# Turned attention probabilities: from SBUF to SBUF in four transfers instead of through DRAM

## Chip, cores and metric

One core of a Trainium2 chip. The metric is the device time of one execution in microseconds (us), lower is better. The kernel before runs in 1198.78 us, the median of three runs (1196.74 to 1199.55).

## What is computed

A per-sequence LoRA matmul is added to the input, then attention with 32 query heads and 8 key/value heads over a paged cache of 512 keys plus the 128 new ones, and its output projection is added too. Eight sequences of 128 tokens; everything is float32. Cut to what matters:

```python
x = x + einsum('bsi,boi->bso', x, weight[adapter_ids])          # LoRA, 512 x 512
q = rope(rmsnorm(einsum('bsd,ed->bse', x, Wq)))                  # 8 x 128 x 32 x 128
k = rope(rmsnorm(einsum('bsd,ed->bse', x, Wk)))                  # 8 x 128 x  8 x 128
v = einsum('bsd,ed->bse', x, Wv)
kc, vc = k_cache[block_table], v_cache[block_table]              # 512 cached keys
k_all, v_all = concat([kc, k]), concat([vc, v])                  # 640 keys
scores = einsum('bqhd,bkhd->bhqk', q, k_all) * SCALE             # each kv head serves 4 q heads
scores = where(valid, scores, -1e30)
probs = softmax(scores)
o = einsum('bhqk,bkhd->bqhd', probs, v_all)
x = x + einsum('bse,de->bsd', o, Wo)
```

## The kernel before

**Tiling.** The heads are cut into G = 4 groups of 2 key/value heads and 8 query heads. A *step* i is one group for one sequence: 32 steps, group by group, and in each group the eight sequences. A step has 8 *slots* h, one per query head. The four query heads that share a key/value head j (0 or 1) are a *unit* (i, j), so slots 0 to 3 and 4 to 7 make one unit each, 64 units in all.

**One slot.** TensorE computes the scores of one head, 128 queries x 640 keys (line 1031). VectorE adds the mask, takes the row minimum and moves them to SBUF (line 1041), ScalarE takes the exponential and its row sum (1057), VectorE the reciprocal (1098), GpSimd scales (1105). This gives p, 128 queries on the partitions x 640 keys.

**Turning the probabilities.** The product with the values needs the keys on the partitions. So in the next slot VectorE turns p in blocks of 32 x 32 (`turn_p`, line 871), into the quarter of the tile tp that belongs to that head. A turned block still has its rows on the wrong partitions: block b of 32 query rows lies on partitions 32b to 32b + 31, each with four pieces (a = 0 to 3) of 640 floats, 2,560 bytes. What is wanted is pT: piece a of partition 32b + i at partition 4i + a, in column block b. Before, two transfers on the SP queue do this. `send(u)` (line 887) writes tp to a DRAM tile xp, 128 partitions x 10,240 bytes, whose addresses run so that (i, a) becomes one index. `receive(u)` (line 894) reads it back, 128 partitions x 4 pieces of 2,560 bytes. The loop calls `send` in the slot of the unit's last turn (line 1065), puts `receive` in the list `to_read`, and calls it one slot later (1073 to 1077), after the `receive` of q if there is one. Keys, queries and later groups' weights go through DRAM in the same manner (xk and kT, xq and qT on SP; tw, xw and w on the ACT queue). Of the last unit the turns are done by TensorE, so 63 units take this way.

**Buffers.** tp has two. pT has one for both units of a step in steps 0 to 4; from step 5 on the second unit uses the buffer that held the LoRA weights, so each of the two has its own. xp has three.

**Order.** The order on each engine is written out by hand. What TensorE does beside the scores stands in `main` for each step: the projections of step i + 1 (`pj_kv`, `pj_q`), `values(i - 1, j)` (o from pT, line 559), `output(i - 1)` and, in the first group, the LoRA product. The pieces are spread over the eight slots. From step 6 on, pT of a unit (i, 0) is read around slot 2 of step i + 1 and pT of (i, 1) around slot 4.

**Queues.** SP only issues transfers, in program order: what stands behind a transfer that waits, waits too. ACT (ScalarE) issues the weights' transfers in between its own arithmetic, and they hold that up in the same way. Each of the 552 transfers of SP and ACT takes the next of eight completion signals, in the order in which the program was laid out over both queues, and before it is issued it waits until the transfer eight places before it, the last on the same signal, has landed. The gathers on GpSimd's queue have signals of their own.

**Weights.** The weights of group g + 1 are turned during group g. In the last two steps of a group, ACT reads them back into the tiles w_kv and w_q (line 517, `receive_weights`) as soon as the old ones have been used, and TensorE uses w_q about two slots after its last row was asked for.

Of the kernel before, what the change touches and what calls it, by code (L numbers as in the profile page):

```python
# [11 lines left out]
FP = mybir.dt.float32  # L12
# [6 lines left out]
P = 128  # L19
# [6 lines left out]
REP = HQ // HK  # L26
# [4 lines left out]
Q4 = P // 4  # L31
NC = LA // P
QK = LA // 4
# [19 lines left out]
def lora_then_paged_attention(  # L53
# [18 lines left out]
    nc = tc.nc  # L72
# [3 lines left out]
    def pool(name, bufs=1, **kw):  # L76
        return ctx.enter_context(tc.tile_pool(name=name, bufs=bufs, **kw))
# [14 lines left out]
    xch = pool("xch", 3, space=bass.MemoryType.DRAM)  # L92
# [686 lines left out]

    to_read = []  # L780

    def send_k(i):
        s = st[i]
        tk = work.tile([P, 4, GK, LC * Q4], FP, tag="tk", name=f"tk_{i}")
        for j in range(GK):
            nc.vector.transpose(
                tk[:, :, j, :].rearrange("p a (c k) -> p a c k", c=LC),
                s.kc[:, :, j * D : (j + 1) * D].rearrange("p c (a d) -> p a c d", a=4),
            )
        s.xk = xch.tile([4, P, GK, LC * Q4], FP, tag="xk", name=f"xk_{i}")  # L790
        nc.sync.dma_start(
            out=s.xk.rearrange("b (i a) h x -> (b i) (a h x)", a=4),
            in_=tk.rearrange("p a h x -> p (a h x)"),
        )
# [9 lines left out]
    def send_q(i, n):  # L804
        s = st[i]
        tq = work.tile([P, 4, 4, Q4], FP, tag=f"tq{n}", name=f"tq_{i}_{n}")
        nc.vector.transpose(tq, s.q[n].rearrange("p h (a d) -> p a h d", a=4))
        xq = xch.tile([4, P, 4, Q4], FP, tag=f"xq{n}", name=f"xq_{i}_{n}")
        nc.sync.dma_start(
            out=xq.rearrange("b (i a) h q -> (b i) (a h q)", a=4),  # L810
            in_=tq.rearrange("p a h q -> p (a h q)"),
        )

        def receive():
            s.qT[n] = work.tile([P, 4, 4, Q4], FP, tag=f"qT{n}", name=f"qT_{i}_{n}")
            nc.sync.dma_start(
                out=s.qT[n].rearrange("d b h q -> d b (h q)"),
                in_=xq.rearrange("b d h q -> d b (h q)"),
            )

        to_read.append((now[0], 0, receive))
# [46 lines left out]
    def turn_p(u, r):  # L868
        if r == 0:
            u.tp = turned.tile([P, 4, REP, QK], FP, tag="tp", name=f"tp_{u.i}_{u.j}")  # L870
        nc.vector.transpose(u.tp[:, :, r, :], u.p.pop(r).rearrange("q (a k) -> q a k", a=4))  # L871
# [12 lines left out]
            t[:, 0:LA].rearrange("p (c b q) -> p c b q", c=NC, b=4),  # L884
        )

    def send(u):
        u.scr = xch.tile([4, P, REP * QK], FP, tag="xp", name=f"xp_{u.i}_{u.j}")
        nc.sync.dma_start(
            out=u.scr.rearrange("b (i a) x -> (b i) (a x)", a=4),  # L890
            in_=u.tp.rearrange("p a r k -> p (a r k)"),
        )

    def receive(u):

        pl, tag = (lora, "raw") if u.j and u.i >= B - 3 else (pts, "pT")
        pT = pl.tile([P, 4, REP, QK], FP, tag=tag, name=f"pT_{u.i}_{u.j}")
        nc.sync.dma_start(
            out=pT.rearrange("p b r k -> p b (r k)"), in_=u.scr.rearrange("b p x -> p b x")
        )  # L900
        st[u.i].pT[u.j] = pT

    def run(queue):
        calls = list(queue)
        queue.clear()
        for f in calls:
            f()
# [73 lines left out]
    for i, (g, b) in enumerate(steps):  # L981
# [38 lines left out]
        for h in range(8):  # L1020
            j, r = h // 4, h % 4
# [8 lines left out]
            for lo, hi in ((0, L), (L, LA)):  # L1030
# [7 lines left out]
            p = probs.tile([P, LA], FP, tag="p", name=f"p_{i}_{h}")  # L1038
# [3 lines left out]
                out=p,  # L1042
# [17 lines left out]
            if prev is not None:  # L1060
                u, pr = prev
                if u.i < last or u.j == 0:
                    turn_p(u, pr)
                if pr == REP - 1:
                    send(u)
                    to_read.append((8 * i + h, 1, lambda u=u: receive(u)))
            run(later)
            run(to_write)
            if 8 * i + h in turn_when:
# [10 lines left out]
            if h == (1 if i else 3) and i < last:  # L1080
                send_k(i + 1)
# [7 lines left out]
            while main and (h == 7 or took + main[0][0] / 2 <= share):  # L1089
                cost, f = main.pop(0)  # L1090
# [9 lines left out]
            if i == last and j == 1:  # L1100

                unit.p[r] = probs.tile([P, LA], FP, tag="p", name=f"pk_{h}")
                p = p.rearrange("q (a c i) -> q a c i", a=4, c=NC)
# [79 lines left out]
```

## Time and profile before

| | before |
|---|---|
| median of three runs | 1198.78 us (1196.74 to 1199.55) |
| the profiled execution | 1197.03 us |
| its span, first to last instruction | 1194.7 us |
| granted TensorE clock | 1.00 |
| busy: VectorE / ScalarE / GpSimd | 61% / 44% / 56% of the span |
| DMA engines, mean busy share by queue | SP and ACT's q1 59.6% and q10 12.4%, GpSimd's q0 10.1% |
| moved | 328.02 MB in 187148 packets; HBM read 195.04 MB, written 132.12 MB |
| one step, first group | about 41 us |
| one step, other groups | 34.6 us |

The profile is one execution on the chip. PE is TensorE's matmuls, DVE is VectorE, ACT ScalarE, POOL GpSimd, SP the engine that only issues transfers; a name ending in q is an engine's queue of issues. L1041 is line 1041 of the kernel. An arrow points from what is read to what is written. In a list of waits, the columns are: who waited, for what, us in total, how many times, the longest. In a timeline, the first column is the start in us from the start of the span and the second the duration; for a transfer that is the time its issue took, not its landing. A row of windows has the stretch, its length, PE's busy time, the granted clock, the DMA share and GB/s. A list of DMA issues ends with the median us from issue to landing.

### The profile page before, as it was taken

To read this page: it belongs to the slowest core of one execution; us is meant where nothing else is said; L and a number is where in the kernel's file an instruction comes from. 1 tells how busy PE (TensorE), PEld (TensorE's weight loads), DVE (VectorE), ACT (ScalarE), POOL (GpSimd) and SP (SyncE) were. 2 spreads that over 40 slices of the span, in tenths; PEclk is the share of its full clock that TensorE was granted. 3 is DMA by queue.
4 is the path that set the end of the run, shared out by engine and by line. 5 is a ranking of instruction groups with operands and counts; after the bars stand their busy time and mean duration, and the time that the engine had idled before them with its cause. 6 is when DMAs were issued, how large, how long until landed. Compare 5 with 4: busy or idle time off the path is not lost.

```text
span 1194.7 us, 12971 instructions
## 1 busy us (share of the span) xinstructions
PE 1178.0 (99%) x3412; PEld 576.4 (48%) x3412; DVE 733.6 (61%) x1675; ACT 531.5 (44%) x1648; POOL 674.9 (56%) x781
## 2 busy tenths in 40 slices
PE   7899999999999999999999999999999999999998
PEld 4554455454444444444444444444444444444454
DVE  5566656665566666766566676666657655565651
ACT  4564444444444444444444444444444444444432
POOL 5566455545566556555655556565556556655540
PEclk9999999999999999999999999999999999999999
DMA  8388788877988988888998998888898987777761
GB/s 290 110 278 273 261 292 293 275 261 246 309 289 301 334 303 300 294 270 300 296 303 280 340 313 298 298 278 300 267 319 277 303 285 264 243 255 242 260 222 60
DMA packets 187148, 328.02 MB, mean 275 GB/s; under 512 B 13124, under 2 KB 106052, under 8 KB 178116
## 3 DMA queue, kind: packets, MB, share of 16 engines
q1 hardware_dynamic: 124272, 239.23, 59.6%
q10 hardware_dynamic: 49524, 48.12, 12.4%
q0 software_dynamic: 13280, 39.86, 10.1%
q8 instruction: 27, 0.44, 0.2%
q14 instruction: 45, 0.37, 0.1%
HBM read 195.04 MB, written 132.12 MB: 274 GB/s over the span
## 4 chain that ended last, share of the span: by engine, by line
PE 97%; DMA 1%; ACT 1%; DVE 0%; POOL 0%; issue 0%; ACTq 0%; DVEq 0%; POOLq 0%
PE o L559 23%; PE sc L1031 23%; PE pj_q L559 18%; PE out L559 18%; PE pj_kv L559 9%; PE y L559 2%; PE lw L474 1%; DMA w_q<-xw_q 1%; PE x L474 1%; PE kt L763 1%; PE wt_q L492 0%; PE wt_kv L492 0%; PE qt L772 0%; PE wt_o L492 0%; PE pt L881 0%
## 5 line engine op out<-in xcount | busy, mean ns | idle before, releaser
L1041 DVE CUSTOM_DVE_ANT_0 p<-sc,mask 128x640 f32<-128x640 f32 x256 | 210.9, 824 | 400.5 <-PE sc L1031 400.4
L1057 ACT ACTIVATE p<-p,mn 128x640 f32<-128x640 f32 x256 | 211.6, 827 | 324.6 <-DVE mn L1041 322.4
L1031 PE MATMUL sc<-kT,qT 128*128 128x512 f32 (+1 forms) x1024 | 318.4, 433 | 1.1 <-ACT kT L764 0.8
L1105 POOL TENSOR_SCALAR p<-p,rc 128x640 f32<-128x640 f32 x252 | 201.9, 801 | 183.0 <-DVE rc L1098 181.0
L1031 PEld LDWEIGHTS sc<-kT,qT 128*128 128x128 f32 x1024 | 189.9, 190 | 226.4 <-issue 206.0
L559 PE MATMUL pj_q<-w_q,x1T 128*128 128x512 f32 x512 | 236.9, 593 | 1.4 <-ACT w_q L493 0.7
L559 PE MATMUL o<-pT,vc 128*128 128x512 f32 x512 | 236.9, 593 | 0.0
L559 PE MATMUL out<-w_o,oT 128*128 128x512 f32 (+1 forms) x528 | 234.9, 580 | 0.9 <-ACT oT L838 0.7
L871 DVE STREAM_TRANSPOSE tp<-p 128x640 f32<-128x640 f32 x252 | 211.0, 837 | 4.9 <-POOL p L1105 4.7
L610 POOL DMA_INDIRECT kc<-in_L_cond_k_cache_dram,key_ix x128 | 130.8, 1022 | 32.7 <-issue 32.5
L610 POOL DMA_INDIRECT vc<-in_L_cond_v_cache_dram,val_ix x128 | 127.9, 999 | 31.0 <-issue 30.8
L692 ACT ACTIVATE q<-q,rs 128x128 f32<-128x128 f32 x256 | 81.9, 390 | 139.1 <-POOL q L679 134.5
L559 PEld LDWEIGHTS out<-w_o,oT 128*128 128x128 f32 x528 | 95.7, 190 | 93.5 <-issue 89.9
L559 PEld LDWEIGHTS pj_q<-w_q,x1T 128*128 128x128 f32 x512 | 92.4, 190 | 93.8 <-issue 91.4
L559 PEld LDWEIGHTS o<-pT,vc 128*128 128x128 f32 x512 | 91.9, 190 | 88.6 <-issue 81.3
L559 PE MATMUL pj_kv<-w_kv,x1T 128*128 128x512 f32 x256 | 116.6, 593 | 0.7 <-ACT x1T L476 0.7
L671 POOL TENSOR_TENSOR k<-sw 128x256 f32<-128x256 f32 x31 | 22.9, 739 | 157.1 <-PE kt L763 133.4
L679 POOL TENSOR_TENSOR q<-q,sw 128x512 f32<-128x512 f32 x59 | 74.7, 1266 | 45.0 <-DVE sw L662 44.9
L646 ACT ACTIVATE sq<-pj_q 128x128 f32<-128x128 f32 x256 | 70.8, 277 | 50.4 <-PE pj_q L559 41.5
L687 POOL TENSOR_TENSOR rs<-ss,mhalf 128x6 f32<-128x6 f32 x64 | 77.6, 1212 | 5.3
L559 PEld LDWEIGHTS pj_kv<-w_kv,x1T 128*128 128x128 f32 x256 | 45.9, 190 | 45.6 <-issue 44.7
L559 PE MATMUL o<-pT,vn 128*128 128x512 f32 x128 | 65.4, 593 | 0.0
(123 smaller groups left out, 873.6 us busy)
## 6 DMA issues: line engine op xcount, KB each, us to landing
xp<-tp SPq DMA_DIRECT2D x63, 1280.0 KB, 5.9
pT<-xp SPq DMA_DIRECT2D x63, 1280.0 KB, 7.0
xk<-tk SPq DMA_DIRECT2D x31, 512.0 KB, 7.5
kT<-xk SPq DMA_DIRECT2D x62, 256.0 KB, 6.6
xq<-tq SPq DMA_DIRECT2D x59, 256.0 KB, 4.6
qT<-xq SPq DMA_DIRECT2D x59, 256.0 KB, 5.2
st_q<-in_L_cond_Wq_dram ACTq DMA_DIRECT2D x24, 256.0 KB, 5.3
xw_q<-tw_q ACTq DMA_DIRECT2D x24, 256.0 KB, 4.4
```

The lines of the kernel that those rows point to most:

```text
L474: nc.tensor.transpose(t[:, j, :], blk, ident)
L559: nc.tensor.matmul(y[0], lhsT=lhsT, rhs=rhs, start=(k == 0), stop=(k == len(pieces) - 1))
L610: nc.gpsimd.indirect_dma_start(out=dst[:, c, :], out_offset=None, in_=src, in_offset=bass.IndirectOffsetOnAxis(ap=rows[:, g, at : at + 1], ...
L646: nc.scalar.activation(sq, t[:, h, :], AF.Square, scale=float(D) ** -0.5, accum_out=ss[:, h : h + 1])
L679: add.tensor_tensor(dst, cw, sw[:, 0:heads, :], ALU.add)
L687: nc.gpsimd.tensor_tensor(rs[:, 0:width], ss[:, 0:width], mhalf[:, 0:width], ALU.pow)
L692: nc.scalar.activation(q, q, AF.Identity, scale=rs[:, h : h + 1])
L871: nc.vector.transpose(u.tp[:, :, r, :], u.p.pop(r).rearrange("q (a k) -> q a k", a=4))
L1031: nc.tensor.matmul(sc[:, lo:hi], lhsT=s.qT[j][:, r, :, :].rearrange("d h q -> d (h q)"), rhs=s.kT[j].rearrange("d a c i -> d (a c i)")[:, ...
L1041: nc.vector.tensor_tensor_reduce(out=p, in0=sc[:, 0:LA], in1=masks[i % 2].rearrange("p a c i -> p (a c i)"), scale=1.0, scalar=3.0e38, op0 ...
L1057: nc.scalar.activation(p, p, AF.Exp, bias=unit.mn[:, one], scale=-1.0, accum_out=unit.sm[:, one])
L1105: nc.gpsimd.tensor_scalar(q, p, unit.rc[:, one], 1.0, ALU.mult, ALU.mult)
```

## The change

`send` and `receive` become one function, `move`. It calls `exchange`, which issues four transfers on SP, one for each block b: source partitions 32b to 32b + 31 of tp with all of their four pieces, destination all 128 partitions of pT in column block b. The DRAM tile xp is not used any more. In the loop the call of `send` in the slot of the last turn is gone, and what `to_read` calls one slot later is `move` instead of `receive`. Choice and number of the pT buffers are as they were. SP then issues 4 transfers per unit instead of 2, so there are 678 on the two queues (552 - 126 + 252), and they take the eight signals in the same way.

```diff
+    def exchange(dst, src):
+
+        for b in range(4):
+            nc.sync.dma_start(
+                out=dst[:, b, :].unsqueeze(1), in_=src[Q4 * b : Q4 * b + Q4, :, :]
+            )
+
...
-    def send(u):
-        u.scr = xch.tile([4, P, REP * QK], FP, tag="xp", name=f"xp_{u.i}_{u.j}")
-        nc.sync.dma_start(
-            out=u.scr.rearrange("b (i a) x -> (b i) (a x)", a=4),
-            in_=u.tp.rearrange("p a r k -> p (a r k)"),
-        )
-
-    def receive(u):
+    def move(u):
 
         pl, tag = (lora, "raw") if u.j and u.i >= B - 3 else (pts, "pT")
         pT = pl.tile([P, 4, REP, QK], FP, tag=tag, name=f"pT_{u.i}_{u.j}")
-        nc.sync.dma_start(
-            out=pT.rearrange("p b r k -> p b (r k)"), in_=u.scr.rearrange("b p x -> p b x")
-        )
+        exchange(pT.rearrange("p b r k -> p b (r k)"), u.tp.rearrange("p a r k -> p a (r k)"))
         st[u.i].pT[u.j] = pT
...
                 if pr == REP - 1:
-                    send(u)
-                    to_read.append((8 * i + h, 1, lambda u=u: receive(u)))
+                    to_read.append((8 * i + h, 1, lambda u=u: move(u)))
```

## The prediction

> **What bounds the kernel now.** I read the page's busy times and DMA queues first, then the windows of PE, then the DMA issues, the waits of the SP queue, the timelines of SP and PE around one step, and last the chain of waits at a change of head group.
>
> ```profile
> span 1194.7 us, 12971 instructions
> PE 1178.0 (99%) x3412; PEld 576.4 (48%) x3412; DVE 733.6 (61%) x1675; ACT 531.5 (44%) x1648; POOL 674.9 (56%) x781
> ...
> q1 hardware_dynamic: 124272, 239.23, 59.6%
> q10 hardware_dynamic: 49524, 48.12, 12.4%
> q0 software_dynamic: 13280, 39.86, 10.1%
> ```
>
> ```profile
> core 0: us, PE busy (x), PEclk, DMA share, GB/s
> ...
> 42.00:1190.00 1148.00, 1144.59 (x3263) 1.00 0.83 277
> ```
>
> TensorE is the bound. It idles 16.7 us in all (1194.7 - 1178.0), and only 3.4 us of that (1148.00 - 1144.59) in the stretch from 42 to 1190 us, where the changed transfers run; the clock is already full (1.00). So nothing done to a transfer can win more than 3.4 us there; what it can do is make TensorE wait. The DMA engines are the second busiest thing, 82% by the queues' shares, and so the place where a loss would come from.
>
> **Removed.** Per unit (four heads of one step; 63 units take this way) one write of the turned probabilities to DRAM and one read back:
>
> ```profile
> xp<-tp SPq DMA_DIRECT2D x63, 1280.0 KB, 5.9
> pT<-xp SPq DMA_DIRECT2D x63, 1280.0 KB, 7.0
> ```
>
> ```profile
> SPq L898 <- DMA xp<-tp: 235.9, 53, 8.5
> SPq L889 <- DVE tp L871: 227.2, 42, 12.7
> ```
>
> The first wait is SP standing with the read until the write has landed, 235.9 us in 53 units, 4.5 us each. It goes away. No engine stands behind it that TensorE waits for, so it is worth 0 on the end. The second wait, for the last transpose, stays, but SP now meets it a slot later, when the transpose is mostly done.
>
> In engine time: queue q1 keeps 16 engines busy for 59.6% of 1194.7 = 712 us with 239.23 MB, 2.98 us per MB, so one 1.31 MB pass is 3.9 us and the pair 7.8 us. Over 63 units that is 492 us of the 984 us (82.4%) that all queues take together. The other 492 us are 41.2% of the time, 14.3 us of a 34.6 us step.
>
> **Added.** Four transfers per unit, each 32 partitions x 10,240 bytes onto 128 partitions x 2,560. SP issues 252 instead of 126. One issue costs 0.36 us (the pT issues) to 1.05 us (the four loads of line 193 that took 4.22 us together); four take 1.4 to 4.2 us, against 0.33 + 0.36 before. Take 3.2 us (line 193's other four, 3.15 us).
>
> No row goes from SBUF to SBUF, and none reads 32 partitions, so bounds. *Engine time*: at least 3.9 us per unit, the bytes crossing once at q1's rate; at most 15.6 us, if a quarter of the partitions gives a quarter of the rate. I take 3.9, from the nearest row: pT lands the same 512 pieces of 2,560 bytes on the same 128 partitions. *Landing of the last of four*: at least 7.0 us, pT's median; at most 4 x 6.6 = 26.4 us, if each waits out the one ahead (kT, the slowest 256 KB row on SP). I take 3 x 0.8 + 7.0 = 9.4 us, since the rows overlap: qT and kT are issued 0.5 us apart and land 5.2 and 6.6 us later.
>
> [...]
>
> **Moved.** The write sat in the slot of the last transpose, the read one slot on; all four now sit at the read. What must be on time:
>
> ```profile
> 406.02 0.32 SPq L889 DMA_DIRECT2D xp<-tp  x1
> 408.19 0.37 SPq L816 DMA_DIRECT2D qT<-xq  x1
> 408.66 1.14 SPq L799 DMA_DIRECT2D kT<-xk  x1
> 414.55 0.36 SPq L898 DMA_DIRECT2D pT<-xp  x1
> ...
> 423.07 0.33 SPq L889 DMA_DIRECT2D xp<-tp  x1
> 423.49 0.39 SPq L799 DMA_DIRECT2D kT<-xk  x1
> 431.52 0.36 SPq L898 DMA_DIRECT2D pT<-xp  x1
> ```
>
> ```profile
> 429.79 3.60 PE L559 MATMUL o<-pT,vc 128*128 128x512 f32 x8
> ...
> 439.68 2.74 PE L559 MATMUL o<-pT,vc 128*128 128x512 f32 x6
> ```
>
> The first unit's four can go once kT is issued, 409.8, and are read at 429.8: 20 us. The second's can go at 423.9 and are read at 439.7: 15.8 us (today its read of 431.5, landing 7.1 us on, has 1.1 us to spare). In the first group one buffer holds both units, and the transfer also waits for the last reader: the pT issued at 126.53 is read at 138.98, 12.4 us. All are above 9.4. The source tp is now held until landing: 409.8 + 9.4 = 419.2, and the next unit but one writes it from 426.85 on, 7.6 us later. Behind the burst on SP stand xq (415.00) and xk (431.97), which need DVE's transposes of tq (done 414.8) and tk (done 428.9) anyway; the burst ends by 413.0 and 427.1. If that cover were gone, each would be up to 3.2 us late. So the issues, the burst and the move cost 0 while a unit stays under 12.4 us to land and under (34.6 - 14.3)/2 = 10.2 us of engine time.
>
> **Sum.** 0 on the path; at best 0.7 us back from the two small waits of TensorE for w_q shown below and at 321 us. Span 1194.7, execution 1197.03 (2.3 us outside the span), 1.75 under the median of 1198.78: I predict that median, 1199 us. About 0.2%, 2.4 us, is what a measurement of this kernel can tell from no change; 1196.4 to 1201.2 is this case. Chance 0.43.
>
> **Rival A: the weights at the end of a group come late (chance 0.30).** SP and ACT transfers share eight completion signals, and each waits for the transfer eight before it. The trace has the effect: ACT's copy of oT, which has nothing to do with pT, sat idle until a pT had landed, because an ACT transfer (403.15 us) was queued ahead of it.
>
> ```profile
> ACT oT L838 <- DMA pT<-xp: 1.1, 1, 1.1
> ```
>
> Two transfers become four in a row, so eight back is nearer. The place with no slack is w_q:
>
> ```profile
> 590.33 8.23 DMA w_q<-xw_q
> 598.56 0.14 issue
> 598.69 3.67 PE pj_q L559 x8
> ```
>
> The pair of w_q issued at 590.33 lands as TensorE needs it. Counting back eight in the new order (xq, three w_q, one w_kv, then the burst) it waits for the second of the four, issued about 0.8 us after kT's issue ends at 581.2, so at 582.0. It decides from a landing 8.3 us after issue. At the longest landing of pT, 10.9 us, the loss is 2.6 us, at three group ends 8 us: 1207. A whole landing late, 8.2 us, at all three is 25 us: 1223. Also w_q at 583.42 would wait for the w_q of 578.80 (median landing 7.4, 586.2), 2.8 us; behind it ACT scales q (585.52, 1.28 us) and copies oT (0.56 us), which then ends at 588.0 instead of 587.3 and is read by the second half of the output matmuls at 589.3, so 1.3 us still cover it. For A: no slack, and ACT cannot go past a waiting transfer. Against: between 590 and 600 us the engines are full (share 1.09), and this traffic halves, so w_q should land sooner than 8.2 us.
>
> **Rival B: the narrow source starves the engines (0.21).** From 10.2 us of engine time per unit the DMA, not TensorE, sets the step; each us beyond costs 2 us in each of 31 steps. At the upper bound 15.6 it is (31.2 + 14.3 - 34.6) x 31 = 338 us: 1537. At 10.5 it is 19 us: 1218. For: a quarter of the partitions, a form with no row. Against: 10.2 is 2.6 times the nearest row.
>
> **Rival C: faster (0.06).** The halved traffic removes the small waits: 0.7 us, at most 3.4, 1195.4 on the median's scale. More than 2.4 us needs nearly all of TensorE's idle time in the stretch, much of which is waits for ACT and DVE, and nothing else in its favour but the runs' own spread (1196.74 to 1199.55).
>
> **How the numbers follow.** Slower is A and B, 0.51; same 0.43; faster 0.06. The likeliest single case is no change: 1199, its own range 1196.4 to 1201.2. The range 1195.5 to 1225 holds that case, A (0.30, to 1223), nearly all of C (0.05) and the mild end of B (0.03), 0.81.
>
> **What would show it.** Right: SP's wait for xp gone, the four landing within 10 us of the first issue, q1's share near 40%, step 34.6 us, TensorE idle about 3 us from 42 to 1190. A: TensorE waiting for w_q near 321, 599 and 876 us, ACT idle on a pT transfer just before. B: the same idle in every step, with o waiting for pT and DVE's transposes for tp, DMA share at 1. I am wrong if TensorE waits in every step though the DMA share is low: then a wait that I did not see has taken the removed one's place.

## The result, and the profile after

The changed kernel takes 1228.84 us (median of 4, 1226.03 to 1232.77), the kernel before 1197.86 us in the same runs (median of 4, 1196.74 to 1199.55). The ratio is 1.026, with a 95% interval of 1.0228 to 1.0292: slower by 2.6%. The profiled execution took 1228.33 us, its span is 1226.6 us, 31.9 us more than before.

The head of its page, with the lines that answer to those shown of before:

```profile
span 1226.6 us, 13216 instructions
PE 1186.2 (97%) x3412; PEld 580.8 (47%) x3412; DVE 734.5 (60%) x1675; ACT 531.5 (43%) x1648; POOL 674.4 (55%) x781
...
q1 hardware_dynamic: 118224, 156.66, 49.6%
```

The traffic fell as the change says, q1 from 239.23 to 156.66 MB. Yet q1's share fell only to 49.6%, 608 us, and not to the 40% or so that the prediction named. The 31.9 us are two things: TensorE is idle 40.4 us (1226.6 - 1186.2) instead of 16.7, 23.7 more, and it is busy 8.2 us longer (1186.2 - 1178.0) with the same 3412 matmuls. Its waits, in the changed kernel (who waited, for what, us in total, times, the longest):

```profile
PE sc L1029 <- DMA qT<-xq: 20.3, 5, 8.1
...
PE x L474 <- DMA acc<-in_x_dram: 2.4, 2, 2.1
PE pj_q L559 <- DMA w_q<-xw_q: 1.6, 1, 1.6
```

These three were not there before, but for 0.2 us of the last. They add up to 24.3 us: the turned queries, the input x of the sequence three ahead, and once the weights at the end of a group. The longer busy time shows in the windows by stretch (stretch, length, busy time of PE, PEld, DVE, ACT and POOL, the granted clock, DMA share, GB/s; PEld is TensorE's loading of weights):

```profile
165.00:206.00 41.00, 39.66 (x118) 20.60 (x119) 22.17 (x46) 16.14 (x47) 14.82 (x17) 0.92 0.53 143
206.00:247.00 41.00, 33.64 (x101) 17.23 (x100) 20.27 (x45) 15.07 (x45) 15.60 (x19) 0.88 0.59 176
...
358.00:1190.00 832.00, 832.00 (x2271) 395.64 (x2270) 531.40 (x1224) 366.38 (x1177) 490.24 (x551) 1.00 0.77 210
```

From 358 us on TensorE is busy in all 832.00 us, at full clock. The whole loss lies in the first head group, where a step took about 41 us before. There the granted clock is now 0.88 to 0.96 in four of the eight stretches from 42 to 358 us. One run of eight o matmuls that began at 326.08 us before begins at 358.37 us now, 32.3 us later; at the end of the span it is 31.9.

One place where it happens. First the timeline of SP's issues in the kernel before, at a unit (i, 0) of the first group (start, length of the issue):

```profile
146.39 0.37 SPq L898 DMA_DIRECT2D pT<-xp  x1
148.98 0.37 SPq L816 DMA_DIRECT2D qT<-xq  x1
149.41 0.50 SPq L104 DMA_DIRECT2D acc<-in_x_dram  x1
```

The timeline of PE there, the matmuls that read what was issued:

```profile
156.93 1.24 PE L1031 MATMUL sc<-kT,qT 128*128 128x512 f32 x4
158.01 1.04 PE L474 MATMUL x<-ident,acc 128*128 128x128 f32 x8
158.88 2.74 PE L559 MATMUL o<-pT,vc 128*128 128x512 f32 x6
```

Then the same place in the changed kernel, SP's issues:

```profile
147.57 5.25 SPq L785 DMA_DIRECT2D pT<-tp  x4
152.92 2.89 SPq L823 DMA_DIRECT2D qT<-xq  x1
155.86 2.44 SPq L104 DMA_DIRECT2D acc<-in_x_dram  x1
```

and PE's first matmuls that read the new q (in brackets the idle time before them, and what ended it):

```profile
166.34 2.47 PE L1029 MATMUL sc<-kT,qT 128*128 128x512 f32 x4 [8.09 <-DMA qT<-xq]
```

Before, q's read landed 5.9 us after its issue, at 154.9, and TensorE read it at 156.93: 2.0 us to spare. x landed after 6.5 us, at 155.9, read at 158.01: 2.1 us. pT landed after 6.7 us, at 153.1, read at 158.88: 5.8 us. Now the four of pT take 5.25 us to issue and 13.8 us until the last has landed; q's read is issued 3.9 us later and its landing, in the chain of waits, takes 13.28 us. It is there at 166.2, TensorE waits 8.09 us, and then runs the four score matmuls in 2.47 us instead of 1.24.

In five units, (1, 0) to (5, 0), q's read stands behind the burst, and TensorE waits for q five times. The other four places:

```profile
116.71 1.32 PE L1029 MATMUL sc<-kT,qT 128*128 128x512 f32 x4 [0.31 <-DMA qT<-xq]
217.24 2.47 PE L1029 MATMUL sc<-kT,qT 128*128 128x512 f32 x4 [7.36 <-DMA qT<-xq]
261.87 1.32 PE L1029 MATMUL sc<-kT,qT 128*128 128x512 f32 x4 [0.93 <-DMA qT<-xq]
308.68 2.48 PE L1029 MATMUL sc<-kT,qT 128*128 128x512 f32 x4 [3.61 <-DMA qT<-xq]
```

The bursts ahead of these took 10.8, 12.4, 10.3 and 12.6 us from the first issue to the last landing: where a burst took 12.4 us or more the wait is 3.6 to 8.1 us, where it took 10.3 or 10.8 us it is under 1 us. The four score matmuls took about twice their time behind the three long waits, and 1.32 us behind the two short ones.

What other queues carry is slower there too. In the stretch from 145 to 156 us before, and from 147 to 167 now, the one write of turned weights on the ACT queue landed after 5.6 and 9.0 us, the gathers on GpSimd's queue after medians of 5.0 to 5.9 and 7.1 to 10.5 us.

### The profile page after: what moved, and what is told of

Read it like the earlier page. It is cut to its first block, busy times and chain, and to the rows that moved or that the text cites. A ratio compares the mean times of both kernels' runs of the same rounds, so it can differ in the third digit from the quotient of the medians.

```text
span 1226.6 us, 13216 instructions
## 1 busy us (share of the span) xinstructions
PE 1186.2 (97%) x3412; PEld 580.8 (47%) x3412; DVE 734.5 (60%) x1675; ACT 531.5 (43%) x1648; POOL 674.4 (55%) x781
## 3 DMA queue, kind: packets, MB, share of 16 engines
q1 hardware_dynamic: 118224, 156.66, 49.6%
q10 hardware_dynamic: 49524, 48.12, 12.2%
## 4 chain that ended last, share of the span: by engine, by line
PE 87%; DMA 5%; SPq 2%; DVE 2%; issue 1%; POOL 1%; ACT 1%; ACTq 0%; DVEq 0%; POOLq 0%
PE sc L1029 21%; PE o L559 21%; PE pj_q L559 16%; PE out L559 15%; PE pj_kv L559 9%; DMA qT<-xq 3%; SPq L785 2%; DMA acc<-in_x_dram 1%; PE y L559 1%; PE lw L474 1%; PE x L474 1%; PE kt L763 1%; ACT sq L646 0%; DVE acc L584 0%; DMA w_q<-xw_q 0%
## 5 line engine op out<-in xcount | busy, mean ns | idle before, releaser
L1029 PE MATMUL sc<-kT,qT 128*128 128x512 f32 (+1 forms) x1024 | 322.4, 438 | 21.4 <-DMA qT<-xq 20.3
L687 POOL TENSOR_TENSOR rs<-ss,mhalf 128x6 f32<-128x6 f32 x64 | 77.5, 1212 | 5.3
```

Source lines behind the costliest of these rows:

```text
L687: nc.gpsimd.tensor_tensor(rs[:, 0:width], ss[:, 0:width], mhalf[:, 0:width], ALU.pow)
L1029: nc.tensor.matmul(sc[:, lo:hi], lhsT=s.qT[j][:, r, :, :].rearrange("d h q -> d (h q)"), rhs=s.kT[j].rearrange("d a c i -> d (a c i)")[:, ...
```

## Experiments

All differ from the changed kernel by the few lines shown, except where said. Ratios are to the kernel before, run beside each, with the 95% interval.

**Which group loses.** The first group's units go through DRAM as before; all later ones move directly.

```diff
-                    to_read.append((8 * i + h, 1, lambda u=u: move(u)))
+                    if u.i < B:
+                        send(u)
+                        to_read.append((8 * i + h, 1, lambda u=u: receive(u)))
+                    else:
+                        to_read.append((8 * i + h, 1, lambda u=u: move(u)))
```

> The units of the first head group (steps 0 to 7) go through DRAM again, all later units go in four transfers as in the change. Theory Q (the loss is the read of q that SP issues behind the burst of four in the first group, and it alone): TensorE no longer waits for qT, the clock stays at 1.00, and the time is that of the kernel before within 0.3%, 1195 to 1201 us. Rival S (the narrow source slows the DMA engines for everybody, so every group pays): a good part of the 31 us stays, above 1206 us.

1196.58 us (10 runs), ratio 0.9992 [0.9974, 1.001]. Span 1194.1, no wait for q or x, clock 1.00. The later groups' 47 direct units cost nothing that can be measured; the loss is the first group's alone.

**Which unit of a step.** In the next two the first group is split: in one only the second unit (i, 1) moves directly, in the other only the first, (i, 0).

```diff
-                    if u.i < B:
+                    if u.i < B and u.j == 0:
```

> In the first group only the second unit of each step, (i, 1), moves directly; the first, (i, 0), goes through DRAM; later groups move directly. If the loss comes from what stands BEHIND the burst on SP: behind (i, 1) stands only the write of the next k, behind (i, 0) the read of q and the load of x. So this kernel loses nothing to 3 us: 1196 to 1201 us, no wait of TensorE for q or x, clock 1.00. If each burst of the first group costs by itself (the engines' load, the source tile or the single pT buffer being held longer): half of the loss, 1210 to 1217 us.

1196.25 us (10 runs), ratio 0.999 [0.9973, 1.0006]; TensorE waits for none of the three, clock 1.00.

```diff
-                    if u.i < B:
+                    if u.i < B and u.j == 1:
```

> The other half of e15: in the first group only the first unit, (i, 0), moves directly, the second goes through DRAM. If it is what stands behind the burst: the whole loss, 1222 to 1232 us, TensorE waiting for qT some 4 times (15 us or more) and its clock under 1.00 after the waits. If each burst costs by itself: 1210 to 1217 us.

1231.7 us (2 runs), ratio 1.0274 [1.0227, 1.0321], TensorE's waits:

```profile
PE sc L1045 <- DMA qT<-xq: 19.9, 5, 8.0
```

So the whole loss hangs on the first unit's burst, the one with the reads of q and x behind it. The bursts of the same make at (i, 1) cost nothing: behind them on SP stands only the write of the next k, and o reads pT late enough. In the first of the two kernels the burst issued at 124.19 us is read by o at 138.97, 14.8 us on.

**q ahead of the burst.** In the first group q's read is taken from its own slot and issued just before the four.

```diff
+            if i < B and any(r[1] for r in due):
+                due += [r for r in to_read if r[1] == 0]
+                to_read[:] = [r for r in to_read if r[1]]
```

> The change with one thing moved: in the first group SP issues the read of q before the burst of four, in the same slot. Theory Q: TensorE's 20 us of waiting for qT and the drop of the clock behind it go away. The burst then starts about 3 us later and lands around 16 us after its slot began, where o reads pT 12.4 us after the issue of before, so a smaller wait of o for pT, up to 4 us in five or six steps, can take its place: 1198 to 1222 us. Rival S (the engines are slow for all): the qT wait goes, but other reads and loads take its place and the time stays above 1222 us.

1225.93 us (2 runs), ratio 1.0238 [1.0218, 1.0258]. The wait for q is gone, and another has its place:

```profile
PE x L474 <- DMA acc<-in_x_dram: 17.4, 4, 6.8
```

The load of x is still behind the four (issued at 161.32, after a burst from 155.22 on) and is read soon after. I had expected o's wait for pT in that place, and less time: a miss, because I again looked at one neighbour only. The time lies where rival S had put it, above 1222 us. With x still behind the burst this run cannot tell the two apart.

**q and x both ahead.** The same three lines, and the load of x goes to the ACT queue.

```diff
-                load_x(b + 3)
+                load_x(b + 3, nc.scalar)
```

> In the first group q's read is issued on SP ahead of the burst, and the load of x for step b + 3 goes to the ACT queue, so neither stands behind the burst. My theory (the loss is whatever TensorE needs next from behind a 14 us burst): the waits for qT and for acc both go, TensorE's clock stays at 0.99 or more, and what remains is o waiting for pT by 0 to 4 us in each of five to seven steps: 1197 to 1215 us. If instead the loss is the burst's load on the DMA engines themselves, whatever the queue: x and the weights, now on other queues, come late all the same, 1220 us or more.

1222.87 us (2 runs), ratio 1.0186 [1.0149, 1.0222]: outside the 1197 to 1215 that I gave it. q's wait is gone, and now the burst itself is too late, and smaller waits stand beside it (waits of TensorE; then one link of the chain: start, length, what):

```profile
PE o L559 <- DMA pT<-tp: 9.5, 2, 5.2
...
PE lw L474 <- DMA lraw<-in_L_cond_weight_dram,lora_ix: 2.6, 1, 2.6
PE x L474 <- DMA acc<-in_x_dram: 2.4, 3, 1.3
```

```profile
202.71 13.63 DMA pT<-tp
```

That burst began at 199.28 and landed at 216.3, 17 us on. TensorE's clock is 0.92 to 0.97 in the four stretches from 124 to 288 us, and its busy time 1187.3 us. The time is again in the range of the rival, the burst's load on the DMA engines whatever the queue (1220 us or more), and part of it shows: x on the ACT queue and the gather of LoRA rows on GpSimd's queue (lraw), with no pT on either, come late too. What the place behind the burst costs and what the load costs is not separated by these two runs. Neither of the two orders tried saves the step: with 2.0, 2.1 and 5.8 us to spare in the place shown, a burst that is 7.1 us longer (13.8 - 6.7) can make whichever stands last late.

**Why the burst is long: the number of transfers.** This one is the kernel before, its read from DRAM cut in four.

```diff
-        nc.sync.dma_start(
-            out=pT.rearrange("p b r k -> p b (r k)"), in_=u.scr.rearrange("b p x -> p b x")
-        )
+        for b in range(4):
+            nc.sync.dma_start(out=pT[:, b, :, :].rearrange("p r k -> p (r k)"), in_=u.scr[b])
```

> The kernel before, with the read from DRAM cut into four transfers of 128 x 2,560 bytes. It has one transfer more per unit than the change. Theory Q with W: four transfers from a wide source cost only their issue (4 x 0.4 us), 1196 to 1202 us. Rival N: the number of transfers or the eight signals cost what the change cost, 1215 us or more.

1200.03 us (5 runs), ratio 1.0024 [1.0005, 1.0042]. Four transfers instead of one cost 2.2 us in all, by the interval 0.6 to 5.0, against 31 us for the change.

**The narrow source.** Four transfers from SBUF to SBUF, each from all 128 partitions. It leaves out the regrouping: column block b of tp goes to column block b of pT on the same partition.

```diff
-                out=dst[:, b, :].unsqueeze(1), in_=src[Q4 * b : Q4 * b + Q4, :, :]
+                out=dst[:, b, :], in_=src[:, b, :]
```

> Four transfers per unit of the same size and the same landing places, but each reads its 2,560 bytes from all 128 partitions (column block b of tp) and not from 32; it leaves out the regrouping of the partitions, so the output is not the reference's. Theory Q with the narrow source as the reason for the slow burst (W): the burst lands in 7 to 9 us instead of about 13.8, at the engines' usual 330 GB/s, the wait for qT is gone or below 5 us, 1196 to 1205 us. Rival N (the number of transfers, their issue or their signals make the burst slow): the burst still takes 12 us or more and the time stays at 1220 to 1232 us.

1195.38 us (8 runs), ratio 0.9988 [0.997, 1.0006]. No wait for q; the four ahead of it at the unit shown land within 5.8 us of their first issue.

**Narrow, or neighbours?** As in the changed kernel 32 partitions with four pieces each, but every fourth one. It leaves out the right regrouping of the query rows.

```diff
-                out=dst[:, b, :].unsqueeze(1), in_=src[Q4 * b : Q4 * b + Q4, :, :]
+                out=dst[:, b, :].unsqueeze(1), in_=src[b:P:4, :, :]
```

> The four transfers keep their form (32 source partitions with four pieces each, onto 128), but each takes every fourth partition of tp instead of 32 neighbours; this leaves out the right regrouping of the query rows. [...] If it is that FEW partitions (32) with four pieces each are read, wherever they lie: rate, landing and waits stay, 1225 to 1233 us.

1196.07 us (4 runs), ratio 0.9988 [0.9949, 1.0027]; one transfer of pT lands after 4.3 us at the median instead of 6.4, the four at the unit shown within 7.4 us of their first issue instead of 13.8, there is no wait for q, and q1's share is 36.9%. The same four microseconds of that unit's burst, by windows as above, in the changed kernel:

```profile
149.00:153.00 4.00, 4.00 (x13) 1.94 (x12) 1.75 (x4) 1.01 (x3) 3.37 (x4) 1.00 0.96 171
```

and in this one:

```profile
149.00:153.00 4.00, 4.00 (x13) 1.88 (x12) 1.13 (x5) 2.09 (x8) 3.17 (x5) 1.00 0.94 285
```

The last two columns tell it: the engines were as busy (0.96 and 0.94), but moved 171 GB/s in the one and 285 in the other. A high DMA share said here that the engines held transfers, not that bytes flowed. What made the burst slow is that its 32 source partitions are neighbours.

**Overlapping the halves.** Blocks in the order 0, 2, 1, 3, so that neighbours in the queue read from different halves of the partitions.

```diff
-        for b in range(4):
+        for b in (0, 2, 1, 3):
```

> The changed kernel with the four blocks issued in the order 0, 2, 1, 3. If each transfer alone is held to half the rate by where its 32 partitions lie, neighbours in the queue now lie in different halves (0 to 63, 64 to 127) and can overlap: the burst shrinks from 13.8 to 8 to 10 us, q lands by about 161, and the time falls to 1198 to 1212 us. If the queue works its transfers off one after the other, or if both halves share their paths: no change, 1225 to 1233 us, q landing 13 us after issue.

1223.16 us (2 runs), ratio 1.0188 [1.012, 1.0256]: between the two expectations, and its interval overlaps the changed kernel's. The trace shows some overlap, 197 GB/s in the same window, a q1 share of 46.0% and 11.6 us for the burst of the unit shown instead of 13.8 (8 to 10 expected), and where the chain of waits runs through q's read, that still takes 9.1 to 12.1 us.

**Two queues.** The same order, blocks 0 and 1 on SP, 2 and 3 on the ACT queue.

```diff
-        for b in range(4):
-            nc.sync.dma_start(
+        for b in (0, 2, 1, 3):
+            (nc.sync if b < 2 else nc.scalar).dma_start(
```

> Blocks 0 and 2... here blocks 0 and 1 are issued on SP and 2 and 3 on the ACT queue, in the order 0, 2, 1, 3, so that one transfer from each half of the partitions is in flight at once. If the half that the source lies in sets the rate: the two halves run side by side, pT lands 8 to 10 us after the first issue, SP has only two transfers ahead of q, so q lands about 7 us earlier, and the time is 1197 to 1212 us, unless ACT's own work is held up by its two issues behind DVE's last turn (then ACT idles on DVE in every step and the time is above 1230). If the rate is one limit for all narrow sources: q lands as late as before and the time stays 1222 to 1235 us.

1225.73 us (2 runs), ratio 1.0209 [1.018, 1.0239]. q1 and q10 together hold the engines for 61.8% of 1224.7 = 757 us (33.2% + 28.6%), in the changed kernel 61.8% of 1226.6 = 758 us (49.6% + 12.2%). Spreading the narrow transfers over two queues saved no engine time. q and x are again late (TensorE waits 7.2 and 8.8 us for them), though only two transfers stand before them on SP: q's write xq, issued at 150.88 behind the ACT queue's two of 149.52 and 150.11, takes 6.75 us to land (4.6 at the median before), and q's read waits for it. The burst on one queue held up the other one too.

**A long burst that is not narrow.** The kernel with four wide transfers, and in the first group, behind pT of each unit (i, 0), two writes of tp into a DRAM tile that nobody reads.

```diff
+        if u.i < B and u.j == 0:
+            for n in range(2):
+                xp = xch.tile([P, 4, REP * QK], FP, tag="xp", name=f"xp_{u.i}_{u.j}_{n}")
+                nc.sync.dma_start(out=xp, in_=u.tp.rearrange("p a r k -> p (a r k)"))
```

> The kernel with four transfers from all 128 partitions (which alone ran as fast as before), with the first unit of each step of the first group followed, on SP and ahead of q, by two writes of tp into a DRAM tile that nobody reads: the burst ahead of q is then three passes of 1.31 MB at full rate, about 3 x 3.5 = 10.5 us of engine time and some 13 us to land, like the changed kernel's, but with no narrow source. It leaves out the regrouping. If a burst of that LENGTH ahead of q is what costs, whatever its form: waits for qT of 10 us or more in all, a granted clock under 1.00 after them, 1212 to 1230 us. [...]

1256.1 us (2 runs), ratio 1.0477 [1.0432, 1.0523], above the 1212 to 1230 us that I gave it. TensorE's wait is the changed kernel's, larger, and its clock again 0.88 to 0.97 in the stretches from 124 to 330 us:

```profile
PE sc L1033 <- DMA qT<-xq: 38.1, 5, 8.9
```

A window inside such a burst:

```profile
161.00:165.00 4.00, 4.00 (x13) 1.91 (x12) 1.01 (x4) 2.09 (x12) 3.29 (x4) 1.00 1.08 405
```

At 405 GB/s this burst is not slow. It is wide, and it cost in the same way, long and ahead of q. Its q landed 14.56 to 15.40 us after issue in the first four of the five waits; I had reckoned with 13.

No kernel here that keeps the whole computation beats the one before by more than can be told; the two that keep DRAM for all of the first group, or for its first units, are level with it.

## Why the prediction was wrong

Forecast: 1199 us, most likely no change. Measured: 1228.84, above the range. By its own steps:

- **What bounds it**: right. TensorE had nothing to win, and what the change could do was make it wait.
- **Removed**: right. SP's wait for xp is gone and worth 0, as the kernel with only the later groups direct shows.
- **Moved: this step failed.** "Behind the burst on SP stand xq (415.00) and xk (431.97)" was read off a step of a later group. There q's read goes out ahead of the burst, also after the change, as its SP timeline shows:

```profile
402.57 0.37 SPq L823 DMA_DIRECT2D qT<-xq  x1
...
403.72 5.22 SPq L785 DMA_DIRECT2D pT<-tp  x4
```

  In the first group the order at (i, 0) is the other one, pT 146.39, qT 148.98, x 149.41: in the trace of before, in a step of 41 us that I read only for pT's 12.4 us. By my own 9.4 us the four would have landed at 155.8 (146.39 + 9.4), 1.1 us before TensorE reads the q that is queued behind them; the place could be seen with my own numbers. The runs showed TensorE waiting there for q, 20.3 us in five places. That no loss comes from (i, 1), nor from later groups, and all of it from (i, 0), is shown by the three kernels that send some units through DRAM.
- **Added, landing of the last of four**: mis-sized. 9.4 us taken, 13.8 measured at the unit shown, 9.4 to 12.6 at the others of the first group whose last landing the trace has. Both errors were needed for a loss of this size: behind bursts of 10.3 and 10.8 us the waits for q were 0.93 and 0.31 us. The 13.8 us alone break the 12.4 us bound of the first group by 1.4 us, which is the kind of wait that came when q and x were out of the way.
- **Added, issue**: 3.2 us taken, 4.8 to 5.6 measured in the first group and up to 6.7 later. A row that the prediction itself shows, kT's issue of 1.14 us, was already above the 1.05 us that it took as the dearest.
- **Added, engine time**: 3.9 us per unit taken. Measured: 608 us of q1, less the 220 us that are not pT (712 - 492), over 63 units, 6.2 us. The wide and the spaced source need 3.5 (37.0% of 1193.5 and 36.9% of 1193.6 us). The nearest row had the right bytes and destination and the wrong source.
- **The bounds of the engine time**: at 6.2 us the measurement lies between the row's 3.9 and the upper bound's 15.6, nearer to the row. I used the engine time for the sum over a step alone and did not carry it into the landing of one burst. The spaced source moved 285 GB/s where the neighbours moved 171, the order 0, 2, 1, 3 moved 197, and two queues saved no engine time (757 us of it against 758). Why 32 neighbouring partitions are read more slowly than 32 spaced ones, no run here shows.
- **Rival A** (weights late at three group ends, 8 to 25 us): one wait for w_q of 1.6 us, at one group end. It did not happen in that size. **Rival B** (every step): did not happen, 6.2 us stays under the 10.2 us where it starts (unrounded 10.15, so its 19 us at 10.5 would be 22; nothing hangs on it). Its cause, the source, is the true one, but because the 32 partitions are neighbours, not because they are few, and it acts by the length of one burst, not by the engines' total. **Rival C**: no. What came is none of the three, though the prediction's last line had left a place for it, a wait not seen while the engines are not full; only not in every step.
- **Left out altogether**: the clock. 8.2 of the 31.9 us are TensorE being busy longer with the same matmuls, most of it behind the three waits of 3.6 us or more, where the granted clock fell.

## What to carry to other kernels

Before a transfer on a queue is made longer, list for every stage of the kernel, not for one step that stands for all, what is issued behind it on that queue, and take landing against first use for each. Look at the other queues as well: here the gathers on GpSimd's queue landed after medians of 7.1 to 10.5 us beside the longer burst, 5.0 to 5.9 before. Price an SBUF source by which partitions it reads (here 171 GB/s from 32 neighbours, 285 from 32 spaced ones), not only by its bytes, and carry that into the landing of one burst as well as into the sum of engine time. Here a wait of TensorE of 3.6 us or more cost more than its length, one of under 1 us did not show it.

## Not expected of the hardware

**The clock after a wait.** In the changed kernel, around the wait of 8.09 us that ends at 166.34 (windows, the granted clock is the third column from the right):

```profile
163.00:165.00 2.00, 0.00 (x0) 0.00 (x0) 0.00 (x0) 0.00 (x0) 0.00 (x0) 0.50 0.56 214
...
169.00:171.00 2.00, 2.00 (x9) 1.65 (x8) 2.00 (x5) 1.03 (x2) 0.00 (x0) 0.50 0.00 0
172.00:173.00 1.00, 1.00 (x4) 0.42 (x3) 0.66 (x2) 0.00 (x0) 0.24 (x1) 1.00 0.51 174
```

It fell to half during the wait: the mean from 161 to 163 was 0.61, so the fall was near 161.4, 3.2 us after the wait began. From 171 to 172 its mean was 0.67, so it came back near 171.7, 5.4 us after work began: at half speed that is 2.7 us lost beyond the wait. The matmuls agree: from these scores to the next LoRA matmuls (lw) took 7.2 us (166.34 to 173.56), the same stretch before 4.5 (156.93 to 161.46). With a wait of 4.96 us, in the kernel with q first, the clock was 0.50 too, from 171 to 174 us.

**Engines full at a low rate.** 0.96 of the DMA engines busy at 171 GB/s, for a source of 32 neighbouring partitions, against 0.94 at 285 for 32 spaced ones and 1.01 at 317 for 128, in the same 4 us.

**Issue times.** The issue of a transfer from SBUF to SBUF took 0.64 us at the median and up to 3.83 us in the changed kernel, that of pT from DRAM 0.36 us before.
